# Cross-attention on one core: value products by head pairs with two accumulator banks, and score tiles of three equal products

## The chip, the core and the metric

The kernel runs on one core of one Trainium2 chip. The metric is the device time of one execution in microseconds. Engines are called by the profile's names: PE is TensorE (PEld its weight loads), ACT ScalarE, DVE VectorE, POOL GpSimd, SP the engine that issues most of the DMAs.

## The reference, cut to what matters

```python
# x: (32, 512, 640) float32, ctx: (32, 77, 1024) float32; 20 heads of 32
q = heads(x @ to_q_w)
s = einsum('bhqd,bhkd->bhqk', q, heads(ctx @ to_k_w)) / sqrt(32)
p = softmax(s, axis=-1)
o = merge(einsum('bhqk,bhkd->bhqd', p, heads(ctx @ to_v_w)))
out = o @ to_out_w + to_out_b + x
```

The reference also computes three attentions over the keys behind the 77th. The context has exactly 77 keys, so these sums are empty and add nothing.

## The kernel before, in words

All operands are float32. To keep float32 accuracy with TensorE's `fp32r` operands, each matrix is split into a high part (a copy rounded to `fp32r`) and a low part (the original less the high part). A product is then three products: high with high, high with low, low with high (`PAIRS`). The low with low term is dropped.

**Context stage, 0 to about 300 us.** The 2464 context rows are worked on in five groups of up to 512 (`GROUPS_KV`). Each group is transposed and split, and keys and values are formed for five chunks of 128 columns (four heads each). They are split again and written to scratch memory, `k_dram` (`split_keys`, L208) and `v_dram` (`split_values`, L223). There the value parts of a column stand next to each other, high and low alternating. The split values pass through a tile `vs` with two buffers.

**Main stage.** It consists of 160 slots (`slot`, L665). Slot n = 5 b + j handles chunk j (four heads) of batch item b; I call the 512 queries of one b a batch, so a batch has five slots. The engines' instructions run in the order in which `slot` writes them down. For its own n, a slot does:

- four score tiles `sc` (`scores`, L460), one per 128 queries: 308 columns for four heads of 77 keys. ScalarE needs the maximum of every head first (VectorE, L482), then does four exponentials with row sums (`exps`, L487);
- the queries of n + 1: 15 products of 512 columns into the bank `pq` (`queries`, L433), then `split_q` (L447);
- for n - 1: the reciprocals of the row sums (`sums`, L500, VectorE), the normalisation of the probabilities `pn` (`normalize`, L505, GpSimd), and the transposition of `pn` into `z` (`transpose_p`, L511, VectorE), from where DMAs write it to a scratch tensor `pd`;
- for n - 3 (named `taken`): the probabilities, which came back by DMA as `raw`, are split into `pp`. Chunks 0 and 1 of `pp` hold the high parts of 256 rows (`cast_p`, L534, ScalarE), chunks 2 and 3 their low parts (VectorE, in `rest_p`, L541), and chunk 4 the high parts of the last 64 rows (ScalarE, L544) above their low parts (`last_p`, L549, GpSimd, L552). Then the value products run (`values`, L560) and their sum is split into `at` (`split_a`, L574): a copy on ScalarE out of the bank `pa`, and a subtraction on VectorE;
- a part of the output projection of an earlier batch: two pieces per slot (`piece`, L610), each of four steps of three products of 320 columns. A finished half row block is added to the residual on VectorE (`finish`, L618, L624) and stored when the row is complete;
- for some j, transpositions of the next batch's x (`transpose_x`, L255, VectorE) and its splits (`split_x`, L259, ScalarE and GpSimd), and the bias (`add_bias`, L588, GpSimd).

**Score tiles before.** `split_q` makes a tile `qt` of three blocks. The first is the high part of the query. The second and third hold, in one half of the partitions, the high part of one half and, in the other half, the low part of the other half. `load_keys` (L410) brings the keys of a batch item into two tiles: `kb`, block diagonal, high parts, 308 columns, and `kc`, which fits the mixed blocks, 154 columns for two heads. A score tile is one product of 308 columns and two of 154.

**Value products before.** The 320 rows (four heads of 80 padded keys) stand in chunks of 128, 128 and 64, and `vb` holds the values block diagonal, 32 output columns per head. Eight products of 512 columns gather in one bank `pa`: three for each full chunk, and two for the last, whose `pp` chunk holds high and low parts together:

```python
PASSES = [(t, a, t + c * 2) for t in range(2) for a, c in PAIRS] + [(2, 0, 4), (2, 1, 4)]
```

Each entry says which rows of `vb`, which part of the values, and which chunk of `pp`. Only the last two use chunk 4.

**PSUM.** There are eight banks of 512 columns: three for `sc`, one for `pq`, one for `pa`, three for the projection (`output_bank`, L591).

**Ends.** `end` (L763) takes the last three slots' probabilities and does the last projections; the last three `take` calls stand between projection products.

Of the kernel before, what the change touches and what calls it, by code (L numbers as in the profile page):

```python
# [35 lines left out]
SEGMENTS = []  # L36
for _t in range(3):
    for _i in range(HPC):
        _lo = max(_t * P, _i * KPAD)
        _hi = min((_t + 1) * P, (_i + 1) * KPAD)  # L40
        if _lo < _hi:
            SEGMENTS.append((_t, _lo - _t * P, _i, _lo - _i * KPAD, _hi - _lo))
            if _t == 2:
                SEGMENTS.append((_t, _lo - _t * P + 64, _i, _lo - _i * KPAD, _hi - _lo))
# [6 lines left out]
def kernel(  # L51
# [46 lines left out]
    v_dram = dram.tile([NT + KPAD - NKEY, HPC, NC_, HD, 2], FPR, name="v_dram")  # L98
# [109 lines left out]
    def split_keys(g, j):  # L208
        g0, gn = GROUPS_KV[g]
        ks = kvt.tile([P, 2, G], FPR, tag="ks", name="ks")  # L210
        split(ks[:, 0, :gn], ks[:, 1, :gn], pks.pop(j)[:, :gn])
        engine = nc.gpsimd if g + 1 < len(GROUPS_KV) else nc.sync
        dst = k_dram.rearrange("(h r) c w n -> r c w h n", h=2)[:, j, :, :, g0 : g0 + gn]
        engine.dma_start(dst[:, 0].bitcast(F32), ks[:64, :, :gn].bitcast(F32))
        for half in range(2):
            engine.dma_start(dst[:, 1, half].bitcast(F32), ks[64:, 1 - half, :gn].bitcast(F32))
# [6 lines left out]
    def split_values(g, j, between=None):  # L223

        g0, gn = GROUPS_KV[g]
        na = gn // Q
        vt = kvp.tile([P, G], F32, tag="vt", name="vt", bufs=1)
        nc.vector.transpose(vt[:, :gn], pvs.pop(j)[:, :gn])
        if between is not None:
            between()  # L230
        vs = kvp.tile([P, G // Q, HD, 2], FPR, tag="vs", name="vs", bufs=2)
        split(vs[:, :na, :, 0], vs[:, :na, :, 1], vt[:, :gn].rearrange("p (a d) -> p a d", d=HD))
        dst = v_dram[g0 : g0 + gn, :, j].rearrange("(a t) i d c -> i t a (d c)", t=Q)
        for i in range(HPC):
            nc.sync.dma_start(  # L235
                dst[i].bitcast(F32),
                vs[i * Q : (i + 1) * Q, :na].rearrange("p a d c -> p a (d c)").bitcast(F32),
            )
# [31 lines left out]

    zero = kvt.tile([P, 2, G], FPR, name="zero", tag="ks")[:, 0]
# [45 lines left out]
    def split_wo():  # L317
# [8 lines left out]
        v_dram[NT:].rearrange("n i j d a -> (n i j d a)").rearrange("(p u) -> p u", u=P).bitcast(F32),  # L326
        zero[: (KPAD - NKEY) * HEADS * HD * 2 // P, :P].bitcast(F32),
# [62 lines left out]
    raws, pps, ats, pds, sms, pqs, pas, xrs, pos = ({} for _ in range(9))  # L390

    kbs, vbs, pnb = [], [], []
    for g, (j0, nj) in enumerate(GROUPS):
        kb = main.tile([P, nj, KCOLS], FPR, name=f"kb{g}")
        kc = main.tile([P, nj, 2, KCOLS // 2], FPR, name=f"kc{g}")
        for tile_ in (kb, kc):
            nc.gpsimd.memset(tile_.bitcast(F32), 0.0)
        kbs.append((kb, kc))
# [4 lines left out]
    qts = [main.tile([P, 3, S], FPR, name=f"qt{n}") for n in range(2)]  # L403
    z = main.tile([P, NBLK, NQ, Q], F32, name="z")
    for g, (j0, nj) in enumerate(GROUPS):
        vb = main.tile([P, nj, 3, HPC * HD, 2], FPR, name=f"vb{g}")
        nc.gpsimd.memset(vb.bitcast(F32), 0.0)
        vbs.append(vb)

    def load_keys(b, g, heads=range(HPC)):  # L410
        j0, nj = GROUPS[g]
        kb, kc = kbs[g]
        src = k_dram[:, j0 : j0 + nj, :, b * NKEY : (b + 1) * NKEY].bitcast(F32)
        for i in heads:
            r, half = slice(i * HD, (i + 1) * HD), i % 2 * NKEY
            nc.sync.dma_start(
                kb[r, :, i * NKEY : (i + 1) * NKEY].bitcast(F32), src[r, :, i // 2, :]
            )
            nc.sync.dma_start(kc[r, :, :, half : half + NKEY].bitcast(F32), src[r])

    def load_values(b, g, segments=SEGMENTS):
        j0, nj = GROUPS[g]
        v = v_dram.rearrange("n i j d a -> n j i (d a)")
        for t, r0, i, k0, kn in segments:
            k0 += b * NKEY
            nc.sync.dma_start(
                vbs[g][r0 : r0 + kn, :, t, i * HD : (i + 1) * HD, :]
                .rearrange("p j d a -> p j (d a)")
                .bitcast(F32),
# [17 lines left out]
    def split_q(n):  # L447

        qt, pq = qts[n % 2], pqs.pop(n)
        nc.scalar.copy(qt[:, 0, :], pq)  # L450
        lower, upper = slice(0, 64), slice(64, P)
        halves = ((lower, upper), (upper, lower))
        for w, (r, other) in enumerate(halves):
            nc.scalar.copy(qt[other, 1 + w, :], qt[r, 0, :].bitcast(F32))  # L454
        for w, (r, other) in enumerate(halves):
            nc.vector.tensor_tensor(  # L456
                qt[r, 1 + w, :], pq[r], qt[r, 0, :].bitcast(F32), ALU.subtract
            )

    def scores(n, t):  # L460
        b, j = divmod(n, NC_)
        g = GROUP_OF[j]
        qt, (kb, kc) = qts[n % 2], kbs[g]
        jg = j - GROUPS[g][0]
        sc = ps.tile([P, S], F32, tag="sc", name="sc", bufs=3)
        half = KCOLS // 2
        for m, (cols, keys_) in enumerate(
            (
                (slice(0, KCOLS), kb[:, jg]),
                (slice(0, half), kc[:, jg, 0]),  # L470
                (slice(half, KCOLS), kc[:, jg, 1]),
            )
        ):
            nc.tensor.matmul(  # L474
                sc[:, cols],
                qt[:, m, t * P : (t + 1) * P],
                keys_,
# [33 lines left out]
    def transpose_p(n):  # L511
# [6 lines left out]
        pd = dram.tile([NBLK * Q, S], F32, tag="pd", name="pd", bufs=6)  # L518
        rows = pd.rearrange("(b i) q -> i b q", i=Q)
# [7 lines left out]
    def load_p(n):  # L527
        pd = pds.pop(n)
        raw = late[0].tile([P, 3, S], F32, tag="raw", name="raw", bufs=2)
        nc.sync.dma_start(raw[:, 0:2, :], pd[0 : 2 * P, :].rearrange("(k p) q -> p k q", p=P))  # L530
        nc.sync.dma_start(raw[:64, 2, :], pd[2 * P :, :])
# [26 lines left out]
    PASSES = [(t, a, t + c * 2) for t in range(2) for a, c in PAIRS] + [(2, 0, 4), (2, 1, 4)]  # L558

    def values(n):  # L560
# [3 lines left out]
        pas[n] = late[1].tile([P, S], F32, tag="pa", name="pa", bufs=1)  # L564
        for m, (t, a, c) in enumerate(PASSES):
            nc.tensor.matmul(  # L566
                pas[n],
                vb[:, t, :, a],
                pp[:, c, :],
                start=(m == 0),  # L570
                stop=(m == len(PASSES) - 1),
            )

    def split_a(n):  # L574
# [4 lines left out]
        split(at[:, 0, :], at[:, 1, :], pas.pop(n))  # L579
# [11 lines left out]
    def output_bank(b, t, h):  # L591
        pos[b, t, h] = late[1].tile([P, S], F32, tag="po", name="po", bufs=3)
# [14 lines left out]
    STEPS += [(t, h, j) for t in range(1, NQ) for h in range(2) for j in range(NC_)]  # L607
    closed = []

    def piece(b, i):  # L610
        for t, h, j in STEPS[4 * i : 4 * i + 4]:
# [36 lines left out]
    def take(m):  # L648
        values(m)
        split_a(m)  # L650
# [14 lines left out]
    def slot(n, beside=()):  # L665
# [78 lines left out]
        if len(beside) > 0:  # L744
            context_values(LAST, beside[0], psv)
        if has_out:
# [4 lines left out]
        if taken is not None:  # L751
            split_a(taken)
        for c in xsplits[1]:
            split_x(b + 1, c)
        exps(n, 3, *s)
        if len(beside) > 1:
# [6 lines left out]
    def end():  # L763
# [28 lines left out]
        def begin(i, j0, j1):  # L792
            t, h = divmod(i, 2)
            if j0 == 0:
# [4 lines left out]
                elif i < 7:  # L799
                    output_bank(last, t, h)  # L800
                else:
                    pos[last, t, h] = late[1].tile([P, S], F32, tag="pa", name="po", bufs=1)
# [96 lines left out]
```

## Time and profile before

| quantity | value |
|---|---|
| median of three runs | 1958.72 us (1957.45 to 1960.53) |
| span of the profiled execution | 1956.4 us |
| median less span | 2.3 us |
| PE, PEld busy | 1929.6, 1727.8 us |
| ACT, DVE, POOL busy | 1596.1, 1363.1, 1024.9 us |
| granted PE clock over the span | 0.997 |
| one batch (five slots) in the steady stretch | 51.50 us |

The page gives the span of the profiled execution, from its first to its last instruction, as its only time; the three timed runs lie 1.1 to 4.1 us above it. The busy times overlap each other. A duration in a row of the trace runs from an instruction's start to its end; on all engines the next instruction often starts before that end, so that the distance from start to start is what a queue of such instructions takes. In a row that gathers several instructions, `x12` is their number, and the text in brackets names what ended the idle time before the first of them.

### The profile page before, as it was taken

To read this page: it belongs to the slowest core of one execution; us is meant where nothing else is said; L and a number is where in the kernel's file an instruction comes from. 1 tells how busy PE (TensorE), PEld (TensorE's weight loads), DVE (VectorE), ACT (ScalarE), POOL (GpSimd) and SP (SyncE) were. 2 spreads that over 40 slices of the span, in tenths; PEclk is the share of its full clock that TensorE was granted. 3 is DMA by queue.
4 is the path that set the end of the run, shared out by engine and by line. 5 is a ranking of instruction groups with operands and counts; after the bars stand their busy time and mean duration, and the time that the engine had idled before them with its cause. 6 is when DMAs were issued, how large, how long until landed. Compare 5 with 4: busy or idle time off the path is not lost.

```text
span 1956.4 us, 37549 instructions
## 1 busy us (share of the span) xinstructions
PE 1929.6 (99%) x10652; PEld 1727.8 (88%) x10652; DVE 1363.1 (70%) x2174; ACT 1596.1 (82%) x6370; POOL 1024.9 (52%) x688
## 2 busy tenths in 40 slices
PE   9999997999999999999999999999999999999999
PEld 7787895889989989999999999999999999998998
DVE  4444446677777777777777777777777777777774
ACT  3232248899999999999999999999999999999993
POOL 0211144566556555555555556655655565555555
PEclk9999999999999999999999999999999999999999
DMA  9877869988888889888988888888888888888876
GB/s 187 172 166 214 174 158 209 219 231 227 216 220 226 227 222 233 226 226 224 236 219 235 217 232 226 226 222 234 223 227 225 225 221 228 218 223 226 224 205 190
DMA packets 592537, 423.49 MB, mean 216 GB/s; under 512 B 219567, under 2 KB 501325, under 8 KB 592333
## 3 DMA queue, kind: packets, MB, share of 16 engines
q1 hardware_dynamic: 588461, 409.79, 83.4%
q0 software_dynamic: 3776, 11.15, 2.1%
q8 instruction: 88, 1.44, 0.3%
q14 instruction: 116, 0.95, 0.2%
q10 hardware_dynamic: 96, 0.16, 0.0%
HBM read 245.61 MB, written 175.32 MB: 215 GB/s over the span
## 4 chain that ended last, share of the span: by engine, by line
PE 86%; DMA 6%; SPq 2%; ACT 2%; DVE 2%; issue 2%; POOL 1%; ACTq 0%; DVEq 0%; POOLq 0%
PE po L596 27%; PE pq L439 26%; PE pa L566 14%; PE sc L474 10%; PE pk L192 5%; PE pv L192 4%; DMA raw<-pd 2%; DMA xs<-in_x_dram 1%; DMA pd<-z 1%; SPq L235 1%; DMA k_dram<-ks 1%; POOL pn L507 1%; ACT pp L538 0%; DMA v_dram<-vs 0%; ACT pn L492 0%
## 5 line engine op out<-in xcount | busy, mean ns | idle before, releaser
L492 ACT ACTIVATE pn<-sc,nm 128x77 f32<-128x77 f32 x2560 | 799.2, 329 | 45.2 <-DVE nm L482 32.4
L507 POOL TENSOR_TENSOR pn<-pn,rs 128x1232 f32<-128x1232 f32 x160 | 364.7, 2279 | 646.9 <-DVE rs L502 632.9
L596 PE MATMUL po<-wo_s,at 128*128 128x320 f32 x3840 | 625.9, 312 | 0.1
L439 PE MATMUL pq<-xt,wq_s 128*128 128x512 f32 x2400 | 619.3, 398 | 1.2 <-POOL xt L265 1.2
L596 PEld LDWEIGHTS po<-wo_s,at 128*128 128x128 f32 x3840 | 565.0, 188 | 0.7 <-DVE xr L624 0.3
L492 ACT ACTIVATION_READ_ACCUMULATOR pn<-sc,nm 128x1 f32 x2560 | 529.5, 207 | 0.0
L482 DVE TENSOR_REDUCE nm<-sc 128x4 f32<-128x308 f32 x640 | 294.2, 460 | 308.8 <-PE sc L474 303.9
L439 PEld LDWEIGHTS pq<-xt,wq_s 128*128 128x128 f32 x2400 | 428.4, 189 | 78.3 <-POOL xt L265 2.4
L566 PE MATMUL pa<-pp,vb 128*128 128x512 f32 x1280 | 329.3, 398 | 2.8 <-POOL pp L552 2.4
L566 PEld LDWEIGHTS pa<-pp,vb 128*128 128x128 f32 x1280 | 242.3, 196 | 43.0 <-POOL pp L552 5.3
L514 DVE STREAM_TRANSPOSE z<-pn 128x1280 f32<-128x1280 f32 x160 | 241.3, 1508 | 27.5 <-POOL pn L507 20.9
L545 DVE TENSOR_TENSOR pp<-raw,pp 128x1024 fp32r<-128x1024 f32 x160 | 196.1, 1226 | 71.3 <-ACT pp L538 63.9
L474 PEld LDWEIGHTS sc<-kc,qt 128*128 128x128 f32 x1280 | 211.6, 188 | 26.6 <-ACT qt L454 4.6
L552 POOL TENSOR_TENSOR pp<-raw,pp 64x512 fp32r<-64x512 f32 x160 | 210.5, 1316 | 42.5 <-ACT pp L544 30.6
L474 PE MATMUL sc<-kc,qt 128*128 128x154 f32 x1280 | 223.0, 255 | 4.1 <-DVE qt L456 2.1
L456 DVE TENSOR_TENSOR qt<-pq,qt 64x512 fp32r<-64x512 f32 x320 | 214.5, 670 | 11.7 <-ACT qt L450 7.3
L265 POOL TENSOR_TENSOR xt<-xs,xt 128x512 fp32r<-128x512 f32 x160 | 204.1, 1296 | 32.3 <-ACT xt L264 28.3
L589 POOL TENSOR_TENSOR xr<-xr,bias 128x640 f32<-128x640 f32 x128 | 201.2, 1573 | 9.7
L454 ACT CAST qt<-qt 64x512 fp32r<-64x512 f32 x320 | 198.1, 619 | 9.0
L474 PE MATMUL sc<-kb,qt 128*128 128x308 f32 x640 | 195.3, 305 | 7.4 <-ACT pn L492 6.2
L538 ACT CAST pp<-raw 128x1024 fp32r<-128x1024 f32 x160 | 170.2, 1064 | 17.3 <-DMA raw<-pd 17.1
L104 ACT CAST at<-pa 128x512 fp32r<-128x512 f32 x160 | 94.7, 592 | 75.8 <-PE pa L566 75.4
(44 smaller groups left out, 1542.5 us busy)
## 6 DMA issues: line engine op xcount, KB each, us to landing
pd<-z SPq DMA_DIRECT2D x640, 160.0 KB, 3.5
raw<-pd SPq DMA_DIRECT2D x160, 512.0 KB, 4.3
xs<-in_x_dram SPq DMA_DIRECT2D x128, 320.0 KB, 6.3
xr<-in_x_dram SPq DMA_DIRECT2D x128, 320.0 KB, 3.8
out_dram<-xr SPq DMA_DIRECT2D x127, 320.0 KB, 3.1
raw<-pd SPq DMA_DIRECT2D x160, 128.0 KB, 4.4
v_dram<-vs SPq DMA_DIRECT2D x80, 128.0 KB, 3.0
kc<-k_dram SPq DMA_DIRECT2D x128, 57.8 KB, 4.2
```

Of the source, the lines that this page charges most:

```text
L265: low.tensor_tensor(parts[1], src, parts[0].bitcast(F32), ALU.subtract)
L439: nc.tensor.matmul(pqs[n], wq_s[:, k, a, j * P : (j + 1) * P], xts[b, k][:, c, :], start=(k == 0 and m == 0), stop=(k == NC_ - 1 and m == 2),)
L456: nc.vector.tensor_tensor(qt[r, 1 + w, :], pq[r], qt[r, 0, :].bitcast(F32), ALU.subtract)
L474: nc.tensor.matmul(sc[:, cols], qt[:, m, t * P : (t + 1) * P], keys_, start=(m == 0), stop=(m == 2),)
L482: nc.vector.tensor_reduce(nm, sc[:, :KCOLS].rearrange("p (h k) -> p h k", k=NKEY), AX.X, ALU.max, negate=True)
L492: nc.scalar.activation(pnb[n % 2][:, at, :NKEY], sc[:, i * NKEY : (i + 1) * NKEY], AF.Exp, bias=nm[:, i : i + 1], accum_out=sms[n][:, at : ...
L507: nc.gpsimd.tensor_tensor(pf, pf, rs.unsqueeze(2).to_broadcast([P, NQ * HPC, NKEY]), ALU.mult)
L514: nc.vector.transpose(z.rearrange("p b t j -> p t b j"), pn.rearrange("p (t h) k -> p t (h k)", t=NQ).rearrange("p t (b i) -> p t b i", i=Q),)
L552: nc.gpsimd.tensor_tensor(pp[64:, 4, :], raw[:64, 2, :], pp[:64, 4, :].bitcast(F32), ALU.subtract)
L566: nc.tensor.matmul(pas[n], vb[:, t, :, a], pp[:, c, :], start=(m == 0), stop=(m == len(PASSES) - 1),)
L589: nc.gpsimd.tensor_tensor(xrs[b, t], xrs[b, t], bias, ALU.add)
L596: nc.tensor.matmul(pos[b, t, h][:, :HALF], ats[b * NC_ + j][:, a, t * P : (t + 1) * P], wos[0][:, j, c, h * HALF : (h + 1) * HALF], start= ...
```

## The change

It has two parts, and a few things that follow from them.

**Score tiles.** `split_q` makes a high and a low part only, both with all four heads in place (one copy on ScalarE, one subtraction on VectorE). The keys stand in one tile `kb`, block diagonal, with a high and a low block of 308 columns each. A score tile is three products of 308 columns by `PAIRS`.

**Value products.** The four heads form two pairs. For a pair p, the 160 rows are one full chunk of 128 (t = 0) and a rest of 32, given twice for its high and low parts (t = 1, `pp` chunk 4). `vb` holds, beside each other, the high and the low parts of the values as output columns: the output's partitions 0 to 63 get the products with the high values of the pair's two heads, and 64 to 127 those with the low values. A pair has three passes, and two pairs have two banks of `pa`. `sum_a` then copies the lower-value half out of PSUM (ScalarE, 64 partitions by 1024 columns) and adds it to the other (VectorE, two additions of 64 by 512) into a tile `aw`; `split_a` makes `at` from `aw`, its copy on ScalarE, its subtraction now on GpSimd instead of VectorE.

**What follows.** `pa` takes two PSUM banks and the projection keeps two of its three. The steps of the projection are cut differently over the pieces (`CUTS`): the third piece has two steps and the fourth six. In slots with j = 3 there is one more `finish`, ahead of the fourth score tile. `split_a` stands behind the fourth tile's exponentials; before, it stood ahead of them. `v_dram` holds for each head high, zero and low values, 96 numbers instead of 64; `vs` has one buffer instead of two; `split_keys` writes `k_dram` with one DMA instead of three. The rows of `pd` and `raw` are arranged to fit the pairs; the bytes read are the same.

```diff
 def split_keys(g, j):
-        dst = k_dram.rearrange("(h r) c w n -> r c w h n", h=2)[:, j, :, :, g0 : g0 + gn]
-        engine.dma_start(dst[:, 0].bitcast(F32), ks[:64, :, :gn].bitcast(F32))
-        for half in range(2):
-            engine.dma_start(dst[:, 1, half].bitcast(F32), ks[64:, 1 - half, :gn].bitcast(F32))
+        engine.dma_start(
+            k_dram[:, j, :, g0 : g0 + gn].bitcast(F32), ks[:, :, :gn].bitcast(F32)
+        )
...
 def split_values(g, j, between=None):
-        vs = kvp.tile([P, G // Q, HD, 2], FPR, tag="vs", name="vs", bufs=2)
-        split(vs[:, :na, :, 0], vs[:, :na, :, 1], vt[:, :gn].rearrange("p (a d) -> p a d", d=HD))
+        split(vs[:, :na, 0], vs[:, :na, 2], vt[:, :gn].rearrange("p (a d) -> p a d", d=HD))
...
+    vs = kvp.tile([P, G // Q, 3, HD], FPR, name="vs")
+    nc.gpsimd.memset(vs.bitcast(F32), 0.0)
...
 def split_q(n):
-        nc.scalar.copy(qt[:, 0, :], pq)
-        lower, upper = slice(0, 64), slice(64, P)
-        halves = ((lower, upper), (upper, lower))
-        for w, (r, other) in enumerate(halves):
-            nc.scalar.copy(qt[other, 1 + w, :], qt[r, 0, :].bitcast(F32))
-        for w, (r, other) in enumerate(halves):
-            nc.vector.tensor_tensor(
-                qt[r, 1 + w, :], pq[r], qt[r, 0, :].bitcast(F32), ALU.subtract
-            )
+        split(qt[:, 0, :], qt[:, 1, :], pq)
...
 def scores(n, t):
-        for m, (cols, keys_) in enumerate(
...
+        for m, (a, c) in enumerate(PAIRS):
             nc.tensor.matmul(
-                sc[:, cols],
-                qt[:, m, t * P : (t + 1) * P],
-                keys_,
+                sc[:, :KCOLS],
+                qt[:, a, t * P : (t + 1) * P],
+                kb[:, j - GROUPS[g][0], c],
...
-    PASSES = [(t, a, t + c * 2) for t in range(2) for a, c in PAIRS] + [(2, 0, 4), (2, 1, 4)]
+    PASSES = [(p, t, c) for p in range(2) for t, c in ((0, p), (0, 2 + p), (1, 4))]
...
 def values(n):
-        pas[n] = late[1].tile([P, S], F32, tag="pa", name="pa", bufs=1)
-        for m, (t, a, c) in enumerate(PASSES):
+        pas[n] = late[1].tile([P, 2, S], F32, tag="pa", name="pa", bufs=1)
+        for m, (p, t, c) in enumerate(PASSES):
             nc.tensor.matmul(
-                pas[n],
-                vb[:, t, :, a],
+                pas[n][:, p, :],
+                vb[:, p, t, :],
                 pp[:, c, :],
...
+    def sum_a(n):
+        pa = pas.pop(n)
+        aw = late[0].tile([P, 2, S], F32, tag="aw", name="aw", bufs=1)
+        nc.scalar.copy(aw[:64], pa[64:])
+        for p in range(2):
+            nc.vector.tensor_tensor(aw[64 * p : 64 * p + 64, 0], pa[:64, p], aw[:64, p], ALU.add)
+        aws[n] = aw
...
 def split_a(n):
-        split(at[:, 0, :], at[:, 1, :], pas.pop(n))
+        aw = aws.pop(n)
+        nc.scalar.copy(at[:, 0, :], aw[:, 0])
+        nc.gpsimd.tensor_tensor(at[:, 1, :], aw[:, 0], at[:, 0, :].bitcast(F32), ALU.subtract)
...
-        pos[b, t, h] = late[1].tile([P, S], F32, tag="po", name="po", bufs=3)
+        pos[b, t, h] = late[1].tile([P, S], F32, tag="po", name="po", bufs=2)
...
+    CUTS = (0, 4, 8, 10, 16, 20, 24, 28, 32, 36, 40)
 def piece(b, i):
-        for t, h, j in STEPS[4 * i : 4 * i + 4]:
+        for t, h, j in STEPS[CUTS[i] : CUTS[i + 1]]:
...
 def slot(n, beside=()):
+        if j == 3:
+            finish()
         if has_out:
             s = scores(n, 3)
         finish()
...
         if taken is not None:
-            split_a(taken)
+            sum_a(taken)
         for c in xsplits[1]:
             split_x(b + 1, c)
         exps(n, 3, *s)
+        if taken is not None:
+            split_a(taken)
```

## The prediction

> **What bounds the kernel now.** I read the page first, then the busy time by stages, then the waits of the steady stretch, then one slot of the timeline, engine by engine.
>
> ```profile
> PE 1929.6 (99%) x10652; PEld 1727.8 (88%) x10652; DVE 1363.1 (70%) x2174; ACT 1596.1 (82%) x6370; POOL 1024.9 (52%) x688
> ```
> ```profile
> 1100.00:1300.00 200.00, 200.00 (x1145) 181.28 (x1144) 150.40 (x242) 185.02 (x761) 118.06 (x74) 1.00 0.87 226
> ```
> In the second line, 200 us of steady work, TensorE (first busy column) has no hole and its clock is 1.00; ScalarE (fourth) is at 92%, VectorE (third) at 75%, GpSimd (fifth) at 59%. So TensorE sets the pace now, and ScalarE follows closely. The waits between 420 and 1900 us say how far the others are from TensorE:
> ```profile
> POOL pn L507 <- DVE rs L502: 569.3, 142, 6.7
> ...
> PEld pa L566 <- POOL pp L552: 2.3, 4, 0.9
> PE pa L566 <- POOL pp L552: 0.7, 2, 0.4
> ```
> GpSimd stands idle 569.3/142 = 4.0 us per slot, always for the same thing: the reciprocals on VectorE that release the normalisation. TensorE has waited for GpSimd's last probability part (L552) a handful of times. This pair is what I follow. One slot, engine by engine (start, duration):
> ```profile
> 1013.75 2.04 PE L566 MATMUL pa<-pp,vb 128*128 128x512 f32 x8
> 1015.62 0.30 PE L474 MATMUL sc<-kb,qt 128*128 128x308 f32 x1
> 1015.76 0.35 PE L474 MATMUL sc<-kc,qt 128*128 128x154 f32 x2
> 1015.95 1.97 PE L596 MATMUL po<-wo_s,at 128*128 128x320 f32 x12
> 1017.75 0.30 PE L474 MATMUL sc<-kb,qt 128*128 128x308 f32 x1
> ...
> 1024.05 2.04 PE L566 MATMUL pa<-pp,vb 128*128 128x512 f32 x8
> ```
> ```profile
> 1016.15 0.48 DVE L482 TENSOR_REDUCE nm<-sc 128x4 f32<-128x308 f32 x1 [0.60 <-PE sc L474]
> 1016.66 0.49 DVE L624 TENSOR_TENSOR xr<-po,xr 128x320 f32<-128x320 f32 x1
> 1017.07 0.83 DVE L257 STREAM_TRANSPOSE xs<-xs 128x640 f32<-128x640 f32 x1
> 1017.83 0.65 DVE L105 TENSOR_TENSOR at<-pa,at 128x512 fp32r<-128x512 f32 x1
> 1018.40 0.46 DVE L482 TENSOR_REDUCE nm<-sc 128x4 f32<-128x308 f32 x1
> 1018.97 1.23 DVE L545 TENSOR_TENSOR pp<-raw,pp 128x1024 fp32r<-128x1024 f32 x1
> 1020.11 0.25 DVE L502 RECIPROCAL rs<-sm 128x16 f32<-128x16 f32 x1
> ```
> ```profile
> 1017.88 1.05 ACT L538 CAST pp<-raw 128x1024 fp32r<-128x1024 f32 x1
> ```
> ```profile
> 1020.52 2.28 POOL L507 TENSOR_TENSOR pn<-pn,rs 128x1232 f32<-128x1232 f32 x1 [6.44 <-DVE rs L502]
> 1022.88 1.30 POOL L552 TENSOR_TENSOR pp<-raw,pp 64x512 fp32r<-64x512 f32 x1
> ```
> Read it as a chain from one slot's value products to the next slot's. They start at 1013.75; once ScalarE has copied `at` and done the four exponentials it casts `pp` (1017.88); VectorE's `pp` part follows at 1018.97, the reciprocals behind it at 1020.11, the normalisation at 1020.52, and behind that on GpSimd the last part, done at 1022.88 + 1.30 = 1024.18. The next value products start at 1024.05, and only the 7th and 8th of the eight need that part: 1024.05 + 6 x 0.234 = 1025.46. The chain has 1.3 us to spare. Five slots take 51.50 us (1017.75 to 1069.25), 10.30 each.
>
> **TensorE's own sum.** Start to start, a 512-column product takes 1.875/8 = 0.234 us, a 320-column one 1.795/12 = 0.150, a 308-column one 0.141, a 154-column one 0.092. A score tile goes from 0.141 + 2 x 0.092 = 0.325 to 3 x 0.141 = 0.423: +0.39 per slot of four. The value products go from eight to six: -0.47. Net -0.08: 10.22 us per slot, if TensorE stays the bound.
> The Trainium skill, "TensorE: Matmul & The Clock Gate" (section Back-to-back issue gap), gives N/2.4 + 2.5 ns for a product of N columns. By that estimate 308 columns take 131 ns, 154 take 67 and 512 take 216, scores cost +0.51, values give -0.43, and the slot grows by 0.08 us: 13 us slower instead of 12 faster. The rows decide.
>
> **The other engines, per slot.** ScalarE loses the two 64x512 query copies (2 x 0.62) and the copy of `at` out of PSUM (0.59); it gains a 64x1024 copy out of PSUM and a 128x512 copy of the sum. 64 partitions cost what 128 do (64x512 0.63 at L544, 128x512 0.63 at L264), so 64x1024 lies between 0.63 and 2 x 0.59 = 1.18; I take the 128x1024 row, 1.06. Sum: -1.83 + 1.69 = -0.14. VectorE: two query parts (1.34) become one (0.67), the `at` part (0.67) goes, two 64x512 sums come at the price of L456 (1.34): 0. GpSimd takes the low part of `at`, 1.30 (L265's shape), inside its 4.0 us of idling. Query split: 1.24 us earlier on ScalarE, not awaited. Key loads halve in number, value loads go from 14 to 16 issues per batch with 1.5 times the bytes; queues at 87% carry fewer packets: 0. By busy time nothing overflows.
>
> **But the order costs.** Three edits meet on one chain. (a) Each head pair's passes now run high, low, rest, so the *third* of six products needs GpSimd's last part, not the seventh of eight: needed 4 x 0.234 = 0.94 us earlier. (b) `at` is no longer one copy off PSUM: copy, two VectorE sums, second copy. (c) That second copy stands on ScalarE behind the exponentials and *ahead of the next `pp` cast*; what queues behind it is the cast, hence VectorE's `pp` part, the reciprocals, the normalisation and the last part, and for the last part waits TensorE. GpSimd's idling is therefore no slack.
> I time the loop from one third value product (T3) to the next, all start to start from rows above:
> 1. To the last product 3 x 0.234 = 0.70, then 0.43 to ScalarE (before: 1013.75 + 1.64 + 0.43 = 1015.82, the `at` copy): copy at 1.13. With 1.05 for it and 0.03 to hand over (1017.88 + 1.05 to 1018.97 left 0.04), the sums may start at 2.21.
> 2. On VectorE they stand behind the fourth score maximum. That tile starts 4 x 0.234 = 0.94 after T3, its maximum 0.62 later (0.53 now plus 0.10 for the wider tile): 1.56; it keeps VectorE 0.51, a residual sum 0.41, a transposition of x 0.76 (the rows above). Slots j = 0 and 1 have both: sums at 3.24. j = 4 has the residual only: 2.48. j = 2 and 3: 2.21.
> 3. Two sums 1.37 (L456 as a pair) and 0.04: second copy at 4.65 (j = 0, 1), 3.89 (j = 4). At j = 2 and 3 ScalarE is later: copy 0.95, one split of x 0.52, exponentials 1.22 after 1.13: 3.82.
> 4. To the `pp` cast 0.52 (start to start of 128x512 copies at 1026.61 and 1027.13), to VectorE's part 1.09, to the reciprocals 1.14, to the normalisation 0.40, to the last part 2.36, to TensorE 1.30 + 0.03: 6.84.
> Loops: j = 0 and 1 11.49 each, j = 2 10.66, j = 4 10.73. For j = 3, TensorE's own way is longer: its second projection piece grows from 12 to 18 products (`CUTS`), so 10.22 + 0.90 = 11.12. Sum 55.49 per batch against 51.50: +4.0 us. The same steps on the kernel before (T7, one copy, no sums) give about 9.1, well under 10.30, as the 1.3 us showed.
> 29 batches (2 to 30) run so: +116. Batch 31 has no x to transpose, and batch 1 starts its projections late: +3 together.
>
> **Banks.** Projection has two PSUM banks instead of three. Piece 3 (j = 3) needs both banks that piece 2 closed; their sums now come before the fourth maximum, at T3 + 1.2 at the latest, and piece 3 starts at T3 + 1.37: 0. Piece 7 (j = 0) waits some 0.3 us, inside the loop's hole: 0 while the loop binds.
>
> **Start and end.** The split values have one buffer instead of two: ScalarE waited 6.1 us for it between 50 and 75 us already, and four splits in a row now wait for each write: three further landings of about 3 us (v_dram: 3.0), partly hidden; TensorE has nothing else at 70 us. +5, from 0 to 10. In the tail the two last `at` arrive later by 1.05 + 1.40 + 0.04 + (1.30 - 0.67) = 3.1 us each, less what products hide: +5.5, from 1 to 8.
> Sum on the profiled span: 1956.4 + 116 + 3 + 5 + 5.5 = 2085.9; the median of the runs lies 2.3 above that span, so 2088. Each of 145 loops is good to 0.2 us (29) and the ends to 8: 2050 to 2126 for this case.
>
> **Holes and the clock.** TensorE would idle 0.8 us per slot. Between 300 and 400 us it idled 12.7 us and was granted 0.97; even that would add 0.3 us of work per slot, less than the hole, so 0 here.
> The Trainium skill, the same page (section The HAM clock gate), ties a fall of the clock to an idle window of about 3.4 us; by that the clock stays at 1.00, and the sum is the same.
>
> **Rivals.** A: the loop closes inside TensorE's 10.22. TensorE stays the bound, 148 x 0.08 = 12 us less; 1947, or 1957 if start and end cost what I say. It decides when the loop is 0.9 us shorter than mine on average. For it: the busy sums. Against it: four engines each serve strictly in the order seen at 1016 to 1020. Chance 0.07. B: the last part arrives in time, but the two banks bind: piece 3 waits until VectorE is through z, queries and two sums, 0.9 us per batch, piece 7 0.3, less 5 x 0.08: +0.8 x 30 = 24; 1993 with the ends. Chance 0.08. C: GpSimd's row is the longer: at j = 3 it holds 2.36 + 1.38 + 1.60 + 3 x 1.30 + 1.30 = 10.54, just under the loop; if its operations stretch by a tenth beside VectorE's, +1 us in two slots of five, 60 us more: 2148. Chance 0.07. My forecast has 0.78.
>
> **The numbers.** The range takes the forecast's own, a little widened downwards: 2043 to 2126. 0.2% is about what a measurement of this kernel can tell from no change. Faster by more: 0.05 (most of A); within: 0.03; slower: 0.92.
>
> **What would show it.** Right: TensorE at some 93%, waiting for GpSimd's last part in nearly every slot, 0.4 to 1.3 us each; ScalarE's second copy waiting for the sums at j = 0 and 1; a batch near 55.5 us. Wrong: TensorE without holes (A), or holes at the projections (B), or GpSimd without idling ahead of the normalisation (C).

## The result, and the profile after

The change makes the kernel slower: 2183.65 us (2181.96 to 2184.32, four runs) against 1959.62 us (1957.45 to 1962.01, four runs), a ratio of 1.114 [1.113, 1.116]. The forecast was 2088 us, at most 2126.

The profiled span grew from 1956.4 to 2182.5 us, by 226.1. I split it at TensorE's first value product of a slot, which both traces show:

| part of the span | before | after | difference | forecast |
|---|---|---|---|---|
| start to slot 3 | 306.94 | 359.94 | +53.0 | +5 |
| slot 3 to slot 158 | 1603.5 | 1759.9 | +156.4 | +119 |
| slot 158 to the end | 45.92 | 62.63 | +16.7 | +5.5 |

So 96.6 us were missed: 48 at the start, 37 in the loop, 11 in the tail. The page's busy times and the stretch from 1100 to 1300 us (columns as before: TensorE, weight loads, VectorE, ScalarE, GpSimd, granted clock, DMA share, GB/s) read:

```profile
PE 1959.6 (90%) x10332; PEld 1697.8 (78%) x10332; DVE 1414.8 (65%) x2174; ACT 1545.2 (71%) x6210; POOL 1207.1 (55%) x807
```
```profile
1100.00:1300.00 200.00, 184.18 (x1012) 161.02 (x1012) 141.72 (x218) 161.19 (x665) 128.41 (x85) 1.00 0.83 207
```

TensorE was busy for 200 of 200 us there and is now busy for 184; no other engine is above 81%. Nobody is short of time, and still everybody waits. The waits from 460 to 2100 us (us in total, times, longest) say for whom:

```profile
PEld pa L544 <- POOL pp L530: 202.4, 144, 2.0
POOL pn L485 <- DVE rs L480: 192.1, 145, 1.3
ACT aw L555 <- PE pa L544: 190.6, 144, 1.7
...
PE pa L544 <- POOL pp L530: 138.0, 142, 1.6
```

The pair of the prediction has turned round. GpSimd's idling ahead of the normalisation fell from 4.0 to 192.1/145 = 1.3 us per slot, and TensorE now waits for GpSimd's last part (L552 before, L530 here) in practically every slot, 138.0/142 = 1.0 us. The lines below make a closed ring: TensorE waits for GpSimd, GpSimd for VectorE, VectorE for ScalarE, ScalarE for TensorE. One turn from a slot with j = 0 to the next, engine by engine:

```profile
1235.15 1.20 PE L544 MATMUL pa<-pp,vb 128*128 128x512 f32 x4 [0.57 <-POOL pp L530]
...
1245.16 0.63 PE L544 MATMUL pa<-pp,vb 128*128 128x512 f32 x2
1246.78 1.21 PE L544 MATMUL pa<-pp,vb 128*128 128x512 f32 x4 [0.98 <-POOL pp L530]
```
```profile
1236.44 1.01 ACT L555 COPY aw<-pa 64x1024 f32<-64x1024 f32 x1 [1.63 <-PE pa L544]
...
1239.79 0.62 ACT L566 CAST at<-aw 128x512 fp32r<-128x512 f32 x1 [0.97 <-DVE aw L557]
1240.31 1.05 ACT L516 CAST pp<-raw 128x1024 fp32r<-128x1024 f32 x1
```
```profile
1235.21 0.65 DVE L106 TENSOR_TENSOR qt<-pq,qt 128x512 fp32r<-128x512 f32 x1
...
1237.60 0.83 DVE L256 STREAM_TRANSPOSE xs<-xs 128x640 f32<-128x640 f32 x1
1238.36 1.34 DVE L557 TENSOR_TENSOR aw<-pa,aw 64x512 f32<-64x512 f32 x2
...
1241.39 1.47 DVE L523 TENSOR_TENSOR pp<-raw,pp 128x1024 fp32r<-128x1024 f32 x1 [1.19 <-ACT pp L516]
1242.78 0.24 DVE L480 RECIPROCAL rs<-sm 128x16 f32<-128x16 f32 x1
```
```profile
1235.17 1.57 POOL L577 TENSOR_TENSOR xr<-xr,bias 128x640 f32<-128x640 f32 x1
1240.48 1.29 POOL L567 TENSOR_TENSOR at<-aw,at 128x512 fp32r<-128x512 f32 x1 [3.74 <-ACT at L566]
1243.10 2.28 POOL L485 TENSOR_TENSOR pn<-pn,rs 128x1232 f32<-128x1232 f32 x1 [1.33 <-DVE rs L480]
1245.46 1.26 POOL L530 TENSOR_TENSOR pp<-raw,pp 64x512 fp32r<-64x512 f32 x1
```

Start with the third value product at 1235.15. The `aw` copy starts 1.29 later, the sums 3.21, the second copy 4.64, the `pp` cast 5.16, VectorE's part 6.24, the reciprocals 7.63, the normalisation 7.95, the last part 10.31, and the next third product 11.63. The first two products of the group had been issued at 1245.16 and then nothing happened for 0.98 us.

The five hops of a batch, and what the prediction had for them:

| hop (third product to third product) | forecast | measured |
|---|---|---|
| j = 0 to 1 | 11.49 | 11.63 |
| j = 1 to 2 | 11.49 | 11.69 |
| j = 2 to 3 | 10.66 | 11.06 |
| j = 3 to 4 | 11.12 | 11.62 |
| j = 4 to 0 | 10.73 | 10.91 |
| batch | 55.49 | 56.91 |

In the lines above one operation has grown: VectorE's `pp` part took 1.23 us before and takes 1.47 here, while GpSimd's `at` subtraction (1240.48 to 1241.77) is still running when it starts. At j = 3 it takes 2.02:

```profile
1218.30 2.02 DVE L523 TENSOR_TENSOR pp<-raw,pp 128x1024 fp32r<-128x1024 f32 x1 [0.47 <-ACT pp L516]
```
```profile
1217.94 1.29 POOL L567 TENSOR_TENSOR at<-aw,at 128x512 fp32r<-128x512 f32 x1
```

Both times it ends 1.09 us after GpSimd's operation does: 1241.77 + 1.09 = 1242.86, and 1219.23 + 1.09 = 1220.32. In all 123 parts between 500 and 1900 us this distance is 1.07 to 1.10 us. The part seems to be held until GpSimd is done, and then to run. By groups, from 500 to 1900 us (busy us, mean ns of one, idle before), the part's mean rose from 1226 ns to 1586:

```profile
L523 DVE TENSOR_TENSOR pp<-raw,pp 128x1024 fp32r<-128x1024 f32 x123 | 195.1, 1586 | 132.7 <-ACT pp L516 132.7
...
L567 POOL TENSOR_TENSOR at<-aw,at 128x512 fp32r<-128x512 f32 x123 | 159.1, 1294 | 317.1 <-ACT at L566 180.8 <-issue 136.3
```

The context stage, 0 to 300 us, shows the start. The first view is of the waits, the second TensorE's rows:

```profile
ACT vs L105 <- DMA v_dram<-vs: 74.3, 12, 8.1
...
PE pk L193 <- ACT ct L105: 34.3, 4, 12.8
PE pk L193 <- DVE ks L106: 5.8, 1, 5.8
```
```profile
73.58 1.65 PE L193 MATMUL pk<-ct,wk_s 128*128 128x512 f32 x3 [5.78 <-DVE ks L106]
83.49 26.39 PE L193 MATMUL pk<-ct,wk_s 128*128 128x512 f32 x105 [8.26 <-ACT ct L105]
```

ScalarE waited there 74.3 us, in 12 waits, for `v_dram` writes to let go of the one `vs` buffer. Before, TensorE's waits for `ct` in this stretch came to 2.4 us; now they are 34.3.

### The profile page after: what moved, and what is told of

Its sections match the earlier page's. It is cut to its first block, busy times and chain, and to the rows that moved or that the text cites. A ratio compares the mean times of both kernels' runs of the same rounds, so it can differ in the third digit from the quotient of the medians.

```text
span 2182.5 us, 36539 instructions
## 1 busy us (share of the span) xinstructions
PE 1959.6 (90%) x10332; PEld 1697.8 (78%) x10332; DVE 1414.8 (65%) x2174; ACT 1545.2 (71%) x6210; POOL 1207.1 (55%) x807
## 3 DMA queue, kind: packets, MB, share of 16 engines
q8 instruction: 84, 1.38, 0.3%
## 5 line engine op out<-in xcount | busy, mean ns | idle before, releaser
L567 POOL TENSOR_TENSOR at<-aw,at 128x512 fp32r<-128x512 f32 x160 | 206.9, 1293 | 417.4 <-ACT at L566 255.2
L544 PE MATMUL pa<-pp,vb 128*128 128x512 f32 x960 | 293.6, 415 | 149.7 <-POOL pp L530 146.2
L452 PE MATMUL sc<-kb,qt 128*128 128x308 f32 x1920 | 379.4, 306 | 14.9 <-ACT pn L470 13.3
L452 PEld LDWEIGHTS sc<-kb,qt 128*128 128x128 f32 x1920 | 325.1, 189 | 61.1 <-ACT pn L470 14.7
L523 DVE TENSOR_TENSOR pp<-raw,pp 128x1024 fp32r<-128x1024 f32 x160 | 252.5, 1578 | 173.8 <-ACT pp L516 173.8
L544 PEld LDWEIGHTS pa<-pp,vb 128*128 128x128 f32 x960 | 162.6, 189 | 233.6 <-POOL pp L530 215.1
L555 ACT COPY aw<-pa 64x1024 f32<-64x1024 f32 x160 | 161.9, 1012 | 223.0 <-PE pa L544 214.3
L557 DVE TENSOR_TENSOR aw<-pa,aw 64x512 f32<-64x512 f32 x320 | 216.0, 675 | 30.0 <-ACT aw L555 27.7
L530 POOL TENSOR_TENSOR pp<-raw,pp 64x512 fp32r<-64x512 f32 x160 | 208.1, 1301 | 20.6 <-ACT pp L522 8.6
L193 PE MATMUL pk<-ct,wk_s 128*128 128x512 f32 (+1 forms) x600 | 146.2, 403 | 42.1 <-ACT ct L105 34.3
L193 PEld LDWEIGHTS pk<-ct,wk_s 128*128 128x128 f32 x600 | 119.2, 200 | 67.4 <-ACT ct L105 36.2
```

Source lines behind the costliest of these rows:

```text
L193: nc.tensor.matmul(held[j][:, :gn], w[:, k, a, :], cts[g, k][:, c, :gn], start=(k == 0 and n == 0), stop=(k == NK - 1 and n == 2),)
L452: nc.tensor.matmul(sc[:, :KCOLS], qt[:, a, t * P : (t + 1) * P], kb[:, j - GROUPS[g][0], c], start=(m == 0), stop=(m == 2),)
L523: nc.vector.tensor_tensor(pp[:, 2:4, :], raw[:, 0:2, :], pp[:, 0:2, :].bitcast(F32), ALU.subtract)
L530: nc.gpsimd.tensor_tensor(pp[64:, 4, :], raw[:64, 2, :], pp[:64, 4, :].bitcast(F32), ALU.subtract)
L544: nc.tensor.matmul(pas[n][:, p, :], vb[:, p, t, :], pp[:, c, :], start=(m % 3 == 0), stop=(m % 3 == 2),)
L557: nc.vector.tensor_tensor(aw[64 * p : 64 * p + 64, 0], pa[:64, p], aw[:64, p], ALU.add)
```

## The experiments

Each kernel differs from the changed one by the edit shown, unless it says "on the kernel before".

**Two buffers for the split values.** The room for the second comes from the staging of the weights (one buffer each for the raw and the split weights instead of two).

```diff
-    vs = kvp.tile([P, G // Q, 3, HD], FPR, name="vs")
+    for i in range(2):
+        vss.append(kvp.tile([P, G // Q, 3, HD], FPR, name=f"vs{i}"))
...
+        vs = vss[0]
+        vss.reverse()
```

> The changed kernel with two buffers for the split values `vs` again (to make room, the staging tile `ws` of the weights has one instead of two). Theory, the single buffer holds up the context stage: the first value product, at 359.9 us in the changed kernel and 306.9 in the kernel before, comes at 308 to 322; ScalarE's waits for the writes to v_dram fall from 84.5 us to under 40; the time goes from 2184 to 2139 (2130 to 2147). Rival, the larger transfers (192 KB instead of 128 KB each, 3.9 us to landing instead of 3.0) hold it up whatever the buffers: 2170 to 2184, first value product after 345.

Measured: 2140.1 us (ratio to before 1.091 [1.086, 1.096]), 44 less. The first value product of slot 3 comes at 316.63, and ScalarE's waits for `v_dram` in the stage fall to 12.1 us.

**One buffer on the kernel before**, to see the same step from the other side.

```diff
-        vs = kvp.tile([P, G // Q, HD, 2], FPR, tag="vs", name="vs", bufs=2)
+        vs = kvp.tile([P, G // Q, HD, 2], FPR, tag="vs", name="vs", bufs=1)
```

> The kernel before with one buffer for the split values instead of two, all else as before. Theory, that buffer alone holds up the context stage, a little less than in the changed kernel since each write is 128 KB and lands in 3.0 us instead of 3.9: the first value product moves from 306.9 us to 335 to 355, the time to 1960 + 38 = 1998 (1988 to 2008). Rival, it needs the changed kernel's larger writes as well: under 1975.

Measured: 2002.1 us (1.020 [1.017, 1.023]), 40 more than the kernel before beside it (1962.4). The first value product comes at 352.82, and the wait from 0 to 300 us is the same:

```profile
ACT vs L104 <- DMA v_dram<-vs: 61.5, 12, 7.0
```

Both together settle 40 to 44 of the 53 us: it is the buffer, and not the new layout of the values, which this kernel lacks. Left over are 316.63 - 306.94 = 9.7 us that I did not take apart; the smaller staging of the weights may be part of them.

**The products that need the last part go last**, as they did before: first the four with full chunks, then the two rests.

```diff
-    PASSES = [(p, t, c) for p in range(2) for t, c in ((0, p), (0, 2 + p), (1, 4))]
+    PASSES = [(p, 0, c) for p in range(2) for c in (p, 2 + p)] + [(p, 1, 4) for p in range(2)]
```

> The changed kernel with the six value passes in another order: high and low of both pairs first, the two rests last, so that GpSimd's last part is needed by the fifth pass instead of the third. Theory, the loop from third pass to third pass through ScalarE, VectorE and GpSimd sets the slot: every slot that waits gets shorter by 2 x 0.234 = 0.47 us, a batch goes from 56.9 to about 54.6 us, the time to 2184 - 29 x 2.3 = 2116 (2105 to 2130). Rival, another wait stands close behind (the projection's banks, z on VectorE): batch above 56.3, time 2165 to 2184.

Measured: 2118.6 us (1.080 [1.075, 1.085]), 65 less; a batch is 54.74 us, forecast 54.6. TensorE's rows show what it is:

```profile
1157.91 1.09 PE L544 MATMUL pa<-pp,vb 128*128 128x512 f32 x4
1159.50 0.73 PE L544 MATMUL pa<-pp,vb 128*128 128x512 f32 x2 [0.50 <-POOL pp L530]
```

Four products are now done before the wait instead of two. The ring is the same, but 2 x 0.23 us of it are used, in each slot. The order of the passes was thus a price of its own, and (a) of the prediction is shown.

**The low part of `at` on VectorE**, in place of GpSimd.

```diff
-        nc.gpsimd.tensor_tensor(at[:, 1, :], aw[:, 0], at[:, 0, :].bitcast(F32), ALU.subtract)
+        nc.vector.tensor_tensor(at[:, 1, :], aw[:, 0], at[:, 0, :].bitcast(F32), ALU.subtract)
```

> The changed kernel with the low part of `at` on VectorE, as before the change, instead of GpSimd. Theory, GpSimd's subtraction stands in the way of VectorE's `pp` part, which read two SBUF operands in 1.23 us before and in 1.47 to 2.02 now: the `pp` part takes 1.23 us in every slot, a batch gets shorter by 4 x 0.25 + 0.4 = 1.4 us (VectorE's own extra 0.6 us fits ahead of the `pp` part), time 2184 - 41 = 2143 (2130 to 2152). Rival, the `pp` part is slow for a reason of its own (its DMA'd operand, the new layout): it stays at 1.4 to 2.0 us and the time at 2175 to 2200.

Measured: 2159.4 us (1.101 [1.096, 1.106]), 24 less, where 41 were expected. The groups from 500 to 1900 us:

```profile
L523 DVE TENSOR_TENSOR pp<-raw,pp 128x1024 fp32r<-128x1024 f32 x125 | 151.8, 1214 | 0.0
```

The `pp` part is back at 1214 ns, in every slot: it was GpSimd's subtraction that held it. But the subtraction, 0.69 us, now stands ahead of the part in VectorE's own queue, and at j = 3 it is held in its turn. GpSimd is splitting x there until 1207.31, and VectorE's subtraction takes 1.16 us and ends 0.55 after that:

```profile
1206.70 1.16 DVE L567 TENSOR_TENSOR at<-aw,at 128x512 fp32r<-128x512 f32 x1 [1.01 <-ACT at L566]
```
```profile
1203.51 3.80 POOL L264 TENSOR_TENSOR xt<-xs,xt 128x512 fp32r<-128x512 f32 x3
```

A batch is 56.17 us, 0.75 less. The cause is confirmed, the size of the remedy was not.

**The same, and `split_a` behind the next slot's first exponentials**, so that the second copy no longer stands ahead of the `pp` cast.

```diff
         exps(n, 3, *s)
         if taken is not None:
-            split_a(taken)
+            pending.append(taken)
...
         exps(n, 0, *s)
+        while pending:
+            split_a(pending.pop())
```

> As the run with the low part of `at` on VectorE, and besides the whole split of `at` (ScalarE's second copy and the subtraction) moved behind the first exponentials of the next slot, so that the `pp` cast no longer stands behind it. Theory, the second copy ahead of the cast is the main part of the loop: the loops fall to 9.7 to 10.2 us, TensorE is the bound again at 10.2 to 10.3 per slot, a batch takes 51.3 to 52.3 us, the time is 2184 - 29 x 5.1 = 2035 (2020 to 2055). Rival, the place of the copy does not matter because ScalarE or VectorE is late anyway: as the run with VectorE alone, 2130 to 2152.

Measured: 2244.3 us (1.144 [1.139, 1.150]), 61 *more* than the changed kernel: the expectation was wrong by over 200 us. The groups from 500 to 1900 us, then one slot on VectorE and on GpSimd:

```profile
L567 DVE TENSOR_TENSOR at<-aw,at 128x512 fp32r<-128x512 f32 x119 | 258.6, 2173 | 95.3 <-ACT at L566 95.3
```
```profile
1212.11 2.12 DVE L567 TENSOR_TENSOR at<-aw,at 128x512 fp32r<-128x512 f32 x1 [0.85 <-ACT at L566]
```
```profile
1211.40 2.28 POOL L485 TENSOR_TENSOR pn<-pn,rs 128x1232 f32<-128x1232 f32 x1 [5.58 <-DVE rs L480]
```

The subtraction starts while GpSimd normalises, and ends at 1214.23, again 0.55 us after GpSimd's operation (1213.68). What takes 0.69 us alone takes 2173 ns on average. VectorE cannot serve the score maxima meanwhile, and ScalarE waits for them 368.3 us in all (460 to 2100 us). It was a bad remedy for a second reason, too. TensorE's waits for the last part did fall, from 138.0 to 37.6 us (460 to 2100 us), but its projection products now waited 67.8 us for the late `at` and 36.2 us for a bank that a sum into `xr` on VectorE had not yet read. The granted clock from 500 to 1900 us was 0.98. How the 61 us divide among these was not tried. What the run does show in its clearest form is the hold: with the changed kernel and the run before, there are three different pairs of operations, and each time VectorE's operation ends a fixed time after GpSimd's.

**`split_a` late in three of the five slots, on GpSimd as in the change** (j = 3, 4 and 0); the call behind the next slot's first exponentials is as above.

```diff
-            split_a(taken)
+            if has_out and ahead and j in (3, 4, 0):
+                pending.append(taken)
+            else:
+                split_a(taken)
```

> The changed kernel with the whole split of `at` (ScalarE's second copy and GpSimd's subtraction) moved behind the first exponentials of the next slot, for the slots j = 3, 4 and 0 only, whose `at` the next projection pieces do not need; the subtraction stays on GpSimd, where it now follows the last part. Theory, the copy ahead of the `pp` cast and GpSimd's subtraction beside VectorE's `pp` part are what lengthens those loops: they fall from 11.6, 10.9 and 11.6 us to TensorE's own 11.2, 10.25 and 10.3; a batch takes 54.5 to 55.0 us, the time 2184 - 62 = 2122 (2105 to 2132). Rival, a later `at` itself is what cost time when all slots had it late: 2175 or more.

Measured: 2101.3 us (1.071 [1.068, 1.074]), 82 less, 21 better than expected. TensorE's six value products are unbroken in those three slots, at 1131.64, 1141.70 and 1152.09, and the two others still wait:

```profile
1109.95 1.20 PE L544 MATMUL pa<-pp,vb 128*128 128x512 f32 x4 [1.28 <-POOL pp L530]
...
1121.02 1.21 PE L544 MATMUL pa<-pp,vb 128*128 128x512 f32 x4 [1.59 <-POOL pp L530]
```

A batch is 54.16 us. So with the whole split behind the cast, the ring closes inside TensorE's own time in these slots. The edit moves two things at once: the second copy, which is (c) of the prediction, and GpSimd's subtraction, which held the `pp` part. That part's mean is 1334 ns now: 1.22 us in two slots, 1.28 in one (a split of x holds it a little), 1.47 in the two unmended. The hold in the three slots was worth at most 0.25 + 0.25 + 0.74 = 1.2 us of the 2.8 us by which the batch became shorter; I put the rest, 1.5 us, down to the copy's place. That is an estimate from rows; (c) was not tried by itself. Nor was (b), the way by two sums, for which there are only the rows above.

**The score part alone**, on the kernel before: its `split_keys`, `load_keys`, `split_q` and `scores` in place of the old ones.

> The kernel before with the score part of the change alone (two query parts, three products of 308 columns, keys in one tile); value products as before. Theory, there TensorE stays the bound and pays 0.39 us more per slot: 10.30 to 10.69, 148 slots, 1960 + 58 = 2018 (2008 to 2030), without waits for GpSimd's last part. Rival, the lighter ScalarE (1.24 us per slot) gives some of it back: under 2000.

Measured: 1986.9 us (1.012 [1.009, 1.015]), 25 more; 55 or so were expected. TensorE has no hole in the stretch from 1100 to 1300 us, and a batch is 52.75 us, so this part costs TensorE 0.25 us per slot and not 0.39:

```profile
1100.00:1300.00 200.00, 200.00 (x1120) 181.84 (x1119) 132.76 (x217) 156.88 (x701) 113.39 (x71) 1.00 0.85 219
```
```profile
1204.84 0.59 PE L451 MATMUL sc<-kb,qt 128*128 128x308 f32 x3
1205.26 1.55 PE L432 MATMUL pq<-xt,wq_s 128*128 128x512 f32 x6
1206.64 0.59 PE L451 MATMUL sc<-kb,qt 128*128 128x308 f32 x3
```

The score tile is at its price (1205.26 - 1204.84 = 0.42), but the six query products behind it take 1.38 from start to start, where they take 1.43 behind a 154-column product. The twelve projection products take 1.76 (1203.08 to 1204.84) where they took 1.80. Part of what a 154-column product costs is thus paid by the group behind it. The time grew by less than the batches say because the first value product comes 4.8 us earlier (302.19), for a reason that I did not take apart. Score tiles of three equal products lose time by themselves, and free ScalarE (185 to 157 us of 200).

**The value part alone**: the changed kernel with the four score functions of the kernel before.

> The changed kernel with the score part undone (query parts in three blocks, one product of 308 columns and two of 154), the value part kept. TensorE has 0.39 us less to do per slot, ScalarE 1.24 us more. Theory, TensorE is not the bound with the value part in place: the time does not fall; ScalarE's extra copies come into the loop in slots j = 2 and 3, some 1 us per batch: 2205 (2175 to 2225). Rival, TensorE's work still counts: 2184 - 58 = 2126 (2110 to 2140).

Measured: 2235.8 us (1.139 [1.135, 1.143]), 52 more than the whole change, where 21 were expected. TensorE has less to do in it, and the time does not fall: its work is not what makes the changed kernel slow. The score part, though a loss by itself, makes up for some of the value part's loss. Of 54.5 us between the two profiled spans, 15.1 lie ahead of the first value product (375.02 against 359.94) and 37.7 between slots 3 and 158; a batch takes 58.0 us, 1.1 more, about what the expectation had. What it missed is the start.

In the loop ScalarE has its two query copies again (181 us of 200 busy), but how much of the loss is theirs is not shown, for the clock fell as well. In nearly every batch one hole, at j = 3, lasts 2.2 us:

```profile
1190.48 1.62 PE L567 MATMUL pa<-pp,vb 128*128 128x512 f32 x4 [2.18 <-POOL pp L553]
```

The granted clock was 0.59 from 1190.4 to 1194.0 us, right behind it, and 0.97 from 500 to 1900 us (1.00 in the changed kernel). The four products took 1.42 us (to the score tile at 1191.90), 1.04 in the changed kernel, and the next six, at 1202.40, came without a hole. On that hop TensorE's own work does set the time.

**Three remedies together**: two buffers, the rests last, `split_a` late in three slots.

> Three remedies in one kernel: two vs buffers, the rests of the value products last, and split_a behind the next slot's first exponentials in slots j = 3, 4 and 0. If each loss is a loss of its own: 2184 - 44 for the start; the three slots with the late split_a already run without a wait for the last part, so the rests in last place bring nothing there, and only the two other hops (j = 1 to 2 and 2 to 3) gain, up to the 1.3 to 1.6 us that they still wait, so about 0.47 each as in the run with the rests last: batch 54.16 - 0.9 = 53.2, sum 2101 - 44 - 29 x 0.9 = 2031, from 2020 to 2045. My theory: loop and start are separate, 2031. Rival 1 (the rests in last place collide with the late split_a, because sums and second copy move nearer to the normalisation and the pp part is blocked for longer): 2055 or more. Rival 2 (once these waits are gone the new order is worth its smaller TensorE sum, as the change by busy time alone would have it): under 1965, a batch near 50.5.

Measured: 2039.0 us (1.040 [1.037, 1.043]), 145 less than the changed kernel, of 191 that the three gave singly (44 + 65 + 82); the difference is the overlap of the last two that was expected. A batch is 53.5 us. In the three mended slots the value products are unbroken. In the shortest, from the score tile behind one value group to the next, TensorE has no hole at all:

```profile
1131.70 0.58 PE L457 MATMUL sc<-kb,qt 128*128 128x308 f32 x3
...
1141.78 0.59 PE L457 MATMUL sc<-kb,qt 128*128 128x308 f32 x3
```

That is 10.08 us, against 10.30 before. If every slot had it, the gain would be 148 x 0.22 = 33 us, an estimate and an upper bound: the next slot takes 10.39, because its twelve projection products take 2.11 us (1142.20 to 1144.31) instead of 1.75. That is the wait of some 0.3 us for a bank in piece 7 that the prediction named. No kernel here beats the one before. Against it, this one still loses 9.4 us ahead of the first value product, 53.3 from slot 3 to slot 158 and 17.6 behind that.

## Why the prediction was wrong in size

**Direction, and mechanism of the loop: right.** It named the ring through GpSimd's last part, the waiter, its place in each slot and 0.4 to 1.3 us of waiting (0.4 to 1.6 measured); the runs with the rests last and with the late `split_a` take the ring apart at two of the three places named. TensorE is busy for 90% of the span (93% forecast). Rivals A and B fall: TensorE has holes, and they stand at the value products. Rival C falls by its own sign: GpSimd still idles 1.3 us ahead of each normalisation. It comes close to the truth at j = 3, as told below.

**The start: 5 us forecast, 53 measured. This term fails most.** The prediction counted three landings of about 3 us, once. The trace shows a longer cycle: the split of a chunk starts at 53.69, 62.60, 71.58 and 80.76, 9 us apart, since a split, its four writes of 192 KB and the next split strictly follow each other now. The context has 25 such chunks, and ScalarE waited in 12 of them up to 300 us. In this first group alone TensorE lost 5.78 + 8.26 us, and holes of 8.89, 12.79 and 4.37 us follow at 149, 219 and 279 us. The prediction looked at one group and took the price of it for that of the stage.

**The loop, step 4: "to the reciprocals 1.14".** They come 1.39 after the `pp` part's start at j = 0 and 1.94 at j = 3, for the hold shown above. The prediction put GpSimd's `at` subtraction into 4.0 us of idling, and its 1.30 was right (1.29). But these were the microseconds in which VectorE's `pp` part ran in the kernel before, with nothing on GpSimd beside it in four slots of five (in the fifth, the last 0.14 us of a split of x). I took idle time of an engine for free without asking who runs beside it. Rival C had stretched operations, but GpSimd's; the trace has VectorE's.
The Trainium skill, "SBUF — State Buffer" (section SBUF: two separate sides), says just this: VectorE and GpSimd share a port pair that one of them holds for a whole instruction, and a VectorE operation with two operands in SBUF is blocked by a GpSimd operation that reads SBUF until that has ended. The rows agree: `pp` from `raw` and `pp` is held, while the query part at 1235.21, which reads one operand from the PSUM bank `pq`, takes 0.65 us as ever beside GpSimd's bias (1235.17, 1.57). The prediction did not weigh this rule, which spoke against the change.

**The loop, step 1: the copy at 1.13.** It comes at 1.29: after the wait, four products take 1.04 from the first to the score tile behind them (1235.15 to 1236.19) and not 4 x 0.234 = 0.94. At j = 0 that cost nothing, since the sums wait for VectorE's transposition: the second copy came at 4.64, forecast 4.65. At j = 2 and 3 it counts, and the sums start at 2.33 instead of 2.21.

**The hop from j = 3: "TensorE's own way is longer", 11.12.** It was a ring again, 11.62, and a shorter one. GpSimd works there without a pause from 1211.30 to 1219.23: last part, bias, three splits of x, and the `at` subtraction at the end. The `pp` part is held until then and takes 2.02, and the normalisation follows at 1220.56. Rival C had this row of GpSimd at 10.54, just under the loop, but not the held `pp` part at its end. With the subtraction on VectorE the hop is still 11.42, since the splits of x hold that instead.

**TensorE's own sum: 10.22, measured 10.08 in a slot without holes.** The value part's -0.47 is right, the score part is +0.25 and not +0.39 (10.30 + 0.25 - 0.47 = 10.08). It made no difference to the time while the ring binds.

**The tail: 5.5, measured 16.7.** The forecast had the late `at` only. The two largest waits are for PSUM banks, whose price the prediction took as 0 in the loop and did not look at in the tail:

```profile
2140.03 4.21 PE L584 MATMUL po<-wo_s,at 128*128 128x320 f32 x18 [3.56 <-DVE xr L613]
...
2169.76 8.80 PE L584 MATMUL po<-wo_s,at 128*128 128x320 f32 x48 [2.66 <-DVE aw L557]
```

The first waits for a bank whose sum into `xr` stands behind the `pp` part on VectorE (2139.56, behind 2138.02); the second takes over the banks of `pa` and waits until VectorE's last two sums have read them. Together they are 6.2 of the 11.2 us missed; the rest I did not take apart. In the loop the price of 0 for the banks held: 10.4 us in 29 waits between 460 and 2100 us, inside the ring's time.

**The clock: right in the loop, wrong at the start.** With holes of 1 us it stayed at 1.00. In the context stage, with holes of 6 to 13 us, it was 0.88 from 50 to 150 us (1.00 before); the 105 products behind the hole of 8.26 us took 26.39/105 = 0.251 us each, where 0.230 (23.89/104) was usual at that place before. The idle window that the prediction cites agrees with both: the loop's holes are shorter than it, these are longer. The run of the value part alone does not fit it: there a hole of 2.2 us, shorter than that window, was followed by a granted clock of 0.59, in nearly every batch.

## What to carry to other kernels

A step that is moved into another engine's idle time is priced by what runs beside it at that moment: look which operations were alone before, above all VectorE's with two SBUF operands when the new work is GpSimd's. Where engines pass one item round in a fixed order, time the whole ring, and count for each edit the place in the queue and not only the busy time; here TensorE stood idle for 8% of the steady stretch, with no other engine above 81%. A buffer count that goes from two to one makes fill, write and landing strictly follow each other: take the whole cycle (9 us here, not the landing of 3 alone) and count over the whole stage how many uses stand closer together than that. Here ScalarE waited in 12 of 25, for 74.3 us, and the time grew by 40 to 44.

## What the runs showed of the hardware that I had not expected

- VectorE's elementwise operation with two SBUF operands waits for a running GpSimd operation to end: 1.23 us became 1.47 to 2.02, and 0.69 became 1.16 to 2.12. It ended 1.07 to 1.10 us (128x1024) and 0.54 to 0.56 us (128x512) after GpSimd's did, in 123 and 119 cases in two runs. An operation with one operand in PSUM showed no such hold (0.65 us).
- It goes the other way too: GpSimd's last part took 1.59 us instead of 1.28 where it started (1213.76) while VectorE's held subtraction was at work (until 1214.23).
- Three 308-column products in place of one of 308 and two of 154 cost TensorE 0.25 us per four tiles, not 0.39: six 512-column products took 1.38 us behind 308 columns and 1.43 behind 154.
- Four value products took 1.04 us after waits of 0.57 and 0.98 us (1235.15 to 1236.19, 1246.78 to 1247.82), 0.94 in an unbroken stream.
- Holes of up to 1.6 us once per slot left the granted clock at 1.00 (changed kernel, 500 to 1900 us). Where one hole per batch was 2.2 us long (value part alone), the clock behind it was 0.59 for 3.6 us.
